# A two-layer graph network on one core: step 2's exponentials and search passes one slot later in the period

## The chip, the core and the metric

The kernel runs on one core of one Trainium2 chip. The metric is the device time of one execution in microseconds (us). The engines are TensorE (PE, with its weight loads PEld), VectorE (DVE), ScalarE (ACT), GpSimd (POOL) and SyncE (SP), which issues most of the DMAs.

## The reference, cut to what matters

The input is x (2708 x 256) and a sparse weighted adjacency matrix adj (2708 x 2708, about 0.3% of it nonzero, with the diagonal). Layer 0 is a graph convolution with a residual and a layer norm. Layer 1 has two attention steps with a nucleus (top-p) cut, beside two steps with the row-normalized adjacency:

```python
def _top_p_attention(X, W1, W2, W3):
    q = X @ W1.T @ W2.T
    k = X @ W3.T
    probs = jax.nn.softmax(q @ k.T, axis=-1)
    idx = jnp.argsort(-probs, axis=-1)
    sp = jnp.take_along_axis(probs, idx, axis=-1)
    cs = jnp.cumsum(sp, axis=-1)
    mask = ... # keep where cs - sp < 0.9
    A = probs * mask
    return A / A.sum(-1, keepdims=True)
R = (adj + eye) / row sums
for n in range(2):
    A = _top_p_attention(Xa, W1, W2, W3)
    Xf = R @ Xf
    Xa = A @ Xa
    Z = Z + Xf @ U1[n].T + Xa @ U2[n].T
x1 = layernorm(X + Z) * ln_g + ln_b
out = layernorm(X + x1)
```

## The kernel before

**Tiling.** The 2708 rows are 22 blocks (NB) of 128, the last one with 20 rows (EDGE). An attention step works on one block of 128 x 2708 exponentials at a time, which lie in one of four buffers es[0] to es[3].

**Stages.** Up to about 300 us layer 0 runs; from there to about 790 us step 1 of layer 1; from about 790 us step 2, the loop `for per in range(NB + 1)`, up to the last final stages. The change touches this loop alone.

**Step 2's loop.** One pass of the loop is called a period, and it is divided into NG = 6 slots (g = 0 to 5). Five blocks are under way in a period:

- block per - 1 (t_mul) is multiplied: `turn` (L520) transposes four 128 x 128 pieces of its kept exponentials on PE into a tr buffer (L526), ACT copies them into wT (L529, L532), and `products` (L552) multiplies them by ya on PE (L563), one slot behind;
- block per (b_dve) is cut on DVE: `last_level` (L959 to L962) takes the search's result, and `finish2` runs one long pass (L976), 20 maxima (L979), the sort (L576, L578), the level (L989 to L1004), five replacements (L1007) and the last pass (L1010); the kernel spreads it over the slots with yields;
- block per + 1 (b_act) is searched for its level on ACT: `try_act` runs a Relu pass (L922), a Sign pass (L925) and small operations (L928 to L938), and all of this twice, for k = 0 and 1. The last of them, L938, leaves the value that last_level reads a period later;
- block per + 2 (b_exp) gets its exponentials: `logits` multiplies queries by keys on PE into the one PSUM buffer lg (L506), in three parts (1024, 1024 and 660 columns), and `exps2` takes the exponential of each on ACT (L818, for the first part also L821 and L822);
- block per + 3 gets the first part of its logits in slot 5; `shift` (L815) takes its maximum on DVE at the start of the next period.

Between these, `r_units` (L718) issues the sparse product of the adjacency on PE (L730): 16 units a period, whose gathered rows POOL fetches by indirect DMA (L698). `r_out` and `arrive` on DVE (L753, L768) take up its results. From per = 10 on, r_units works on its second round, and from about per = 12 the final stages follow: the statistics on DVE (L1037), a Sqrt on ACT in slot 5 (L1087), the norm on ACT in slot 0 (L1047, after DVE's L1089 and L1090), POOL's scale and shift (L1062, L1063), the stores on SP (L1070).

**Order.** The schedule is written by hand: each engine runs its instructions in the order of the program, and waits only where an operand or a buffer asks for it. tr, wT and the accumulators have two buffers each; lg has one, so a logits call waits until the exponentials of the part before have read it. At per = 0 there is no turn and no b_exp; b_exp exists for per = 1 to 19, b_act for per = 0 to 20.

Of the kernel before, what the change touches and what calls it, by code (L numbers as in the profile page):

```python
# [52 lines left out]
def gnn_two_layer_kernel(ctx: ExitStack, tc: tile.TileContext, N, xT_d, x_d, adj_d, w0_d, b0_d,  # L53
# [71 lines left out]
    with fast:  # L125
        fast_path(fast, tc, c, flags, fint, xT_d, x_d, w0_d, b0_d, w1_d, w2_d, w3_d, u1_d, u2_d, g_d, b_d)
# [22 lines left out]
def fast_path(ctx, tc, c, flags, fint, xT_d, x_d, w0_d, b0_d, w1_d, w2_d, w3_d, u1_d, u2_d, g_d, b_d):  # L149
# [19 lines left out]
    def ps_acc(t=None):  # L169
        acc = ps.tile([P, CH], FP, tag="acc", name="acc")  # L170
        if t == NB - 1:
            nc.vector.memset(acc[:, :D + 1], 0.0)
        return acc
# [324 lines left out]
    def logits(s, t, i):  # L498


        p = rows(t)
        lg = ps_lg()
        cs = CHS[2 * i:2 * i + 2]
        for h, (a, b) in enumerate(cs):
            o = slice(DA * h, DA * h + DA)
            nc.tensor.matmul(lg[:p, h, :b - a], lhsT=q[o, t * P:t * P + p], rhs=keys[s][o, i, :b - a],  # L506
                             start=True, stop=True)
        a, b = cs[0][0], cs[-1][1]
        return lg.rearrange("p h n -> p (h n)")[:p, :b - a], a, b
# [42 lines left out]
    def products(keep):  # L552

        if len(before) > keep:
            p, ks, wT, y, acc = before.pop(0)
            for k in ks:
                kw = rows(k)
                if p < P:
                    o = EW * (k % 4)
                    nc.tensor.matmul(acc[o:o + p, :D], lhsT=wT[:kw, k % 4, :p], rhs=y[:kw, k, :],  # L560
                                     start=k < 4, stop=k >= NB - 4)
                    continue
                nc.tensor.matmul(acc[:p, :D], lhsT=wT[:kw, k % 4, :p], rhs=y[:kw, k, :],  # L563
                                 start=k == 0, stop=k == NB - 1)
# [34 lines left out]
    def exps1(t):  # L599

        p = rows(t)
        e = es[t % 4]
        nmax, srt = st1[t]
        z = small.tile([P, 2], FP, tag="z1", name="z1", bufs=3)
        st1[t] = (srt, z)
        h = 11 * P

        def part(i):
            if i == 0:
                nc.scalar.activation(srt[:p], srt[:p], AF.Exp, bias=nmax[:p], scale=1.0)  # L610
            a, b = ((0, h), (h, N))[i]
            nc.scalar.activation(e[:p, a:b], e[:p, a:b], AF.Exp, bias=nmax[:p], scale=1.0,
                                 accum_out=z[:p, i:i + 1])
        return part
# [103 lines left out]
    def r_units(n):  # L718
        for _ in range(n):
            s, m = r_queue[0]  # L720
            p = rows(m)
            if not r_now:
                r_now[:] = [ps_misc(), 0]
                if m + 1 < NB:
                    r_load(s, m + 1)
            acc, k = r_now
            a, y = r_in[s, m]
            kw = CW if k < CC else p
            rhs = v[:p, m, :] if s and k == CC else y[:kw, k, :]
            nc.tensor.matmul(acc[:p, :D], lhsT=a[:kw, k, :p], rhs=rhs, start=k == 0, stop=k == CC)  # L730
            r_now[1] += 1
            if k == CC:
                r_now.clear()
                r_queue.pop(0)
                r_in.pop((s, m))
                base = za_load(m) if s else None
                later[1].append(lambda s=s, m=m, acc=acc, base=base: r_out(s, m, acc, base))
# [44 lines left out]
    def e2(t):  # L782
        return es[(t + 2) % 4]
# [30 lines left out]
    def shift(b, lg):  # L814
        nc.vector.tensor_reduce(b.nmax, lg[:, :P], AX.X, ALU.max, negate=True)  # L815

    def exps2(b, i, lg, a, c_):
        nc.scalar.activation(e2(b.t)[:b.p, a:c_], lg, AF.Exp, bias=b.nmax, scale=1.0,  # L818
                             accum_out=b.all[:b.p, i:i + 1])
        if i == 0:  # L820
            nc.scalar.activation(b.half, b.nmax, AF.Identity, bias=part_of[:b.p], scale=0.5)  # L821
            nc.scalar.activation(e2(b.t)[:b.p, HC:2 * HC], lg, AF.Exp, bias=b.half, scale=0.5, accum_out=b.roots)  # L822
# [23 lines left out]
    part = exps1(0)  # L846
# [5 lines left out]
    part = exps1(1)  # L852
# [11 lines left out]
    for t in range(NB):  # L864
        acc = ps_acc(t)
        part = exps1(t + 2) if t + 2 < NB else None
# [4 lines left out]
        for g in range(NG):  # L871
# [5 lines left out]
            if b and g in (0, 2):  # L877
                lg = logits(1, b.t, g // 2)
# [239 lines left out]
    lg = logits(1, 3, 0)  # L1118
# [3 lines left out]
    for per in range(NB + 1):  # L1122
        n_r = units.get(per, 0)
        b_act = blocks.get(per + 1)
        b_dve = blocks.get(per)
        t_mul = per - 1 if per else None
        if per:
            accs[t_mul] = ps_acc(t_mul)
        masks = None
        b_exp = None  # L1130
        if per and per + 2 < NB:
            b_exp = blocks[per + 2] = Block(per + 2)
        for g in range(NG):
            n = n_r * (g + 1) // NG - n_r * g // NG
            now = later.pop(0)
            later.append([])
            if g == 0:
                if b_exp:
                    shift(b_exp, lg[0])
                r_units(n)  # L1140
            if t_mul == EDGE:
                if g == 0:
                    products(0)
                    edge_product(ya, accs[EDGE], e2(EDGE))
            elif per:
                turn(t_mul, g, ya, accs[t_mul], e2(t_mul))
            if b_exp and g == 3:
                lg = logits(1, b_exp.t, 2)
            if g == NG - 1 and 3 < per + 3 < NB:
                lg = logits(1, per + 3, 0)  # L1150
            if g:
                r_units(n)
            if b_exp and g == 1:
                lg = logits(1, b_exp.t, 1)
            if t_mul != EDGE:
                products(1 if per else 0)
            if b_exp and g in (0, 1, 3):
                exps2(b_exp, (g + 1) // 2, *lg)
            if b_act:
                for k, part in {0: ((0, 0),), 1: ((0, 1), (0, 2), (0, 3)), 2: ((1, 0),), 3: ((1, 1), (1, 2), (1, 3))}.get(g, ()):  # L1160
                    try_act(b_act, k, part)
            if g == 0:
                if b_dve:
                    last_level(b_dve)
                    masks = finish2(b_dve)
                    next(masks)
                final_slot(0)
                if per > 1:

                    t = t_mul - 1  # L1170
                    base = za_load(t)
                    later[0].append(lambda t=t, base=base: arrive(t, base, accs.pop(t), ras.pop(t)[:rows(t)]))
            elif masks:
                next(masks, None)
                if b_exp and g == 5:
                    begin_search(b_exp)
            for f in now:
                f()
            if g:
                final_slot(g)  # L1180
# [388 lines left out]
```

## Time and profile before

| what | value |
| --- | --- |
| median of 3 runs | 1396.02 us (1394.66 to 1401.23) |
| the profiled execution's own time | 1395.44 us |
| its span, first to last instruction | 1393.4 us |
| granted PE clock, mean | 0.966 |
| step 2's loop, first L976 to last L976 | 800.29 to 1345.34 us |
| a period of it, early (954.03 to 978.49) | 24.46 us |
| a period of it, late (1239.23 to 1266.03) | 26.80 us |
| L922 and L925 on ACT | x43 of 2641 ns, x42 of 2643 ns |
| L818 on ACT | x66, median 1114 ns |
| L506 on PE | x528, median 590 ns |

A profile is taken from one execution. Times in it are microseconds from the start of its span. A row of the timeline has start, duration, engine, line, operation, tiles out<-in, shape and count, and in square brackets the idle time before it and what ended that. A row of the waits has who waited, for whom, the total in us, how often, and the longest. Busy shares are means over the whole span.

### The profile page before, as it was taken

To read this page: it belongs to the slowest core of one execution; us is meant where nothing else is said; L and a number is where in the kernel's file an instruction comes from. 1 tells how busy PE (TensorE), PEld (TensorE's weight loads), DVE (VectorE), ACT (ScalarE), POOL (GpSimd) and SP (SyncE) were. 2 spreads that over 40 slices of the span, in tenths; PEclk is the share of its full clock that TensorE was granted. 3 is DMA by queue.
4 is the path that set the end of the run, shared out by engine and by line. 5 is a ranking of instruction groups with operands and counts; after the bars stand their busy time and mean duration, and the time that the engine had idled before them with its cause. 6 is when DMAs were issued, how large, how long until landed. Compare 5 with 4: busy or idle time off the path is not lost.

```text
span 1393.4 us, 18921 instructions
## 1 busy us (share of the span) xinstructions
PE 1279.4 (92%) x5788; PEld 898.7 (64%) x5788; DVE 1044.1 (75%) x3482; ACT 743.9 (53%) x1340; POOL 645.0 (46%) x595
## 2 busy tenths in 40 slices
PE   8999999988999999999998849999998988898884
PEld 6877877833567666666666437777665766566662
DVE  2544545865888887776751379999999988999996
ACT  1000000035455555555554438888887887899951
POOL 1000000014544532775555286776734757677870
PEclk9999999999999999999999879999999999999997
DMA  6544544512222110232223245545432544345351
GB/s 184 179 152 151 164 147 150 165 36 66 67 91 65 52 56 9 88 101 63 65 64 94 84 132 156 159 146 156 138 98 88 158 137 128 114 147 177 123 146 36
DMA packets 92830, 157.94 MB, mean 113 GB/s; under 512 B 16356, under 2 KB 65196, under 8 KB 92720
## 3 DMA queue, kind: packets, MB, share of 16 engines
q1 hardware_dynamic: 66434, 100.59, 22.7%
q0 software_dynamic: 20544, 51.17, 13.1%
q10 hardware_dynamic: 5742, 4.89, 1.3%
q8 instruction: 48, 0.79, 0.2%
q14 instruction: 62, 0.51, 0.1%
HBM read 125.33 MB, written 31.26 MB: 112 GB/s over the span
## 4 chain that ended last, share of the span: by engine, by line
PE 55%; DVE 36%; issue 3%; ACT 3%; another core or an unknown queue 1%; POOL 1%; DMA 0%; ACTq 0%; DVEq 0%; POOLq 0%
PE acc L563 16%; PE acc L255 15%; PE lg L506 6%; DVE cand L979 6%; DVE w L1007 5%; PE tr L526 5%; DVE e L1010 4%; DVE w L976 4%; PE misc L677 3%; DVE srt L576 3%; DVE spare L578 3%; PE acc L649 2%; PE misc L427 2%; PE acc L461 2%; PE misc L422 2%
## 5 line engine op out<-in xcount | busy, mean ns | idle before, releaser
L529 ACT COPY wT<-tr 128x512 f32<-128x512 f32 (+2 forms) x258 | 131.9, 518 | 242.0 <-PE tr L526 158.6
L563 PE MATMUL acc<-ya,wT 128*128 128x256 f32 (+1 forms) x924 | 235.8, 396 | 12.3 <-ACT wT L529 8.8
L563 PE MATMUL acc<-x,wT 128*128 128x256 f32 (+1 forms) x924 | 233.0, 391 | 6.6 <-ACT wT L529 6.6
L698 POOL DMA_INDIRECT yg<-yf_d,ix x154 | 192.6, 1251 | 95.3 <-PE misc L730 50.2
L698 POOL DMA_INDIRECT yg<-v_d,ix x154 | 194.8, 1265 | 85.5 <-PE tr L526 35.2
L563 PEld LDWEIGHTS acc<-x,wT 128*128 128x128 f32 (+1 forms) x924 | 166.5, 191 | 88.0 <-issue 48.5
L563 PEld LDWEIGHTS acc<-ya,wT 128*128 128x128 f32 (+1 forms) x924 | 172.2, 194 | 67.9 <-issue 26.4
L255 PE MATMUL acc<-y,adj_t 128*128 128x257 f32 (+1 forms) x924 | 208.8, 382 | 0.0
L365 POOL DMA_INDIRECT adj_t<-in_adj,ix x154 | 171.8, 1116 | 50.8 <-issue 39.9
L255 PEld LDWEIGHTS acc<-y,adj_t 128*128 128x128 f32 (+1 forms) x924 | 171.7, 189 | 33.8 <-issue 10.2
L730 PE MATMUL misc<-yg,adj_t 128*128 128x256 f32 (+1 forms) x660 | 174.4, 398 | 13.5 <-DVE v L753 7.0
L506 PE MATMUL lg<-k,q 64*128 64x512 f32 (+3 forms) x528 | 152.5, 601 | 26.9 <-ACT e L822 24.4
L526 PE MATMUL tr<-ident,e 128*128 128x128 f32 (+2 forms) x946 | 150.5, 279 | 19.3 <-DVE e L1010 18.9
L730 PEld LDWEIGHTS misc<-yg,adj_t 128*128 128x128 f32 (+1 forms) x660 | 118.5, 193 | 60.1 <-issue 20.7
L526 PEld LDWEIGHTS tr<-ident,e 128*128 128x128 f32 (+2 forms) x946 | 115.3, 142 | 61.8 <-issue 21.4
L332 POOL DMA_DIRECT2D part_d<-e x1 | 0.6, 573 | 294.5 <-DVE e L331 294.5
L569 DVE MAX8 cand<-e 128x8 f32<-128x170 f32 (+1 forms) x352 | 88.1, 319 | 38.5 <-ACT e L513 28.3
L922 ACT ACTIVATE w<-e,st 128x2708 f32<-128x2708 f32 (+1 forms) x43 | 113.5, 2640 | 0.0
L925 ACT ACTIVATE w<-e,st 128x2708 f32<-128x2708 f32 (+1 forms) x42 | 111.0, 2643 | 0.1
L438 ACT COPY x1T<-tr 128x256 f32<-128x256 f32 (+1 forms) x22 | 8.0, 364 | 192.1 <-PE tr L437 192.1
L979 DVE MAX8 cand<-w 128x8 f32<-128x136 f32 (+1 forms) x440 | 93.5, 284 | 0.8
L576 DVE MAX8 srt<-spare 128x8 f32<-128x128 f32 (+3 forms) x264 | 81.3, 308 | 9.1
(230 smaller groups left out, 1791.7 us busy)
## 6 DMA issues: line engine op xcount, KB each, us to landing
adj_t<-in_adj SPq DMA_DIRECT2D x44, 704.0 KB
adj_t<-adjc_d SPq DMA_DIRECT2D x44, 448.0 KB
adjc_d<-adj_t SPq DMA_DIRECT2D x22, 256.0 KB
base<-za_d SPq DMA_DIRECT2D x41, 128.0 KB
adjc_d<-adj_t SPq DMA_DIRECT2D x22, 192.0 KB
xt<-in_x ACTq DMA_DIRECT2D x21, 128.0 KB
x_d<-x SPq DMA_DIRECT2D x21, 128.0 KB
x1b_d<-xb SPq DMA_DIRECT2D x21, 128.0 KB
```

The costliest lines, as they stand in the source:

```text
L255: nc.tensor.matmul(acc[:p, :n], lhsT=halves[k // KH][:kw, k % KH, :p], rhs=y[:kw, k, :n], start=k == 0, stop=stop and k == NB - 1)
L365: nc.gpsimd.indirect_dma_start(out=a[:CW, i, :], out_offset=None, in_=adj_rows, in_offset=bass.IndirectOffsetOnAxis(ap=ix[:CW, m, i:i + 1] ...
L506: nc.tensor.matmul(lg[:p, h, :b - a], lhsT=q[o, t * P:t * P + p], rhs=keys[s][o, i, :b - a], start=True, stop=True)
L526: nc.tensor.transpose(tr[:kw, k % 4, :p], e[:p, k * P:k * P + kw], ident[:p, :p])
L529: nc.scalar.copy(wT[:, :full, :p], tr[:, :full, :p])
L563: nc.tensor.matmul(acc[:p, :D], lhsT=wT[:kw, k % 4, :p], rhs=y[:kw, k, :], start=k == 0, stop=k == NB - 1)
L576: nc.vector.max(dst[:p, i:i + 8], src[:p])
L698: nc.gpsimd.indirect_dma_start(out=y[:CW, i, :], out_offset=None, in_=rows_d, in_offset=bass.IndirectOffsetOnAxis(ap=ix[:CW, m, i:i + 1], ...
L730: nc.tensor.matmul(acc[:p, :D], lhsT=a[:kw, k, :p], rhs=rhs, start=k == 0, stop=k == CC)
L922: nc.scalar.activation(scr[:b.p, :N], e, AF.Relu, bias=b.nz, scale=b.l[k], accum_out=b.relu)
L925: nc.scalar.activation(scr[:b.p, :N], e, AF.Sign, bias=b.nz, scale=b.l[k], accum_out=b.sign)
L979: nc.vector.max(cand[:p, 8 * i:8 * i + 8], w[:p, SEG2 * i:SEG2 * (i + 1)])
```

## The change

In step 2's loop, the second part of the logits and its exponentials go from slot 1 to slot 2, and the third part from slot 3 to slot 4. The search's passes on ACT go from slots 0, 1, 2 and 3 to slots 1, 2, 3 and 4. The first part of the exponentials stays in slot 0, and the first part of the logits for the block after stays in slot 5. Within a slot the places stay: logits part 2 (the second) stands behind r_units, part 3 (the third) before them.

```diff
-            if b_exp and g == 3:
+            if b_exp and g == 4:
                 lg = logits(1, b_exp.t, 2)
             if g == NG - 1 and 3 < per + 3 < NB:
                 lg = logits(1, per + 3, 0)
             if g:
                 r_units(n)
-            if b_exp and g == 1:
+            if b_exp and g == 2:
                 lg = logits(1, b_exp.t, 1)
             if t_mul != EDGE:
                 products(1 if per else 0)
-            if b_exp and g in (0, 1, 3):
-                exps2(b_exp, (g + 1) // 2, *lg)
+            if b_exp and g in (0, 2, 4):
+                exps2(b_exp, g // 2, *lg)
             if b_act:
-                for k, part in {0: ((0, 0),), 1: ((0, 1), (0, 2), (0, 3)), 2: ((1, 0),), 3: ((1, 1), (1, 2), (1, 3))}.get(g, ()):
+                for k, part in {1: ((0, 0),), 2: ((0, 1), (0, 2), (0, 3)), 3: ((1, 0),), 4: ((1, 1), (1, 2), (1, 3))}.get(g, ()):
                     try_act(b_act, k, part)
```

## The prediction

> **What bounds the kernel now.** I read the page's busy table first, then the waits of VectorE (DVE) and TensorE (PE) in the stretch that the change touches (step 2's loop, about 794 to 1345 us), then single periods of that loop in the timeline.
>
> The page's table names PE as the busiest engine, which is a mean over stages:
>
> ```profile
> PE 1279.4 (92%) x5788; PEld 898.7 (64%) x5788; DVE 1044.1 (75%) x3482; ACT 743.9 (53%) x1340; POOL 645.0 (46%) x595
> ```
>
> Busy time by stage (columns: length, then busy us and count for PE, weight load, DVE, ACT and POOL, clock, DMA), for one early and one late period, each from one L976 to the next:
>
> ```profile
> 954.03:978.49 24.46, 23.18 (x113) 17.11 (x112) 23.45 (x80) 20.01 (x34) 17.75 (x14) 1.00 0.52 152
> 1239.23:1266.03 26.80, 23.94 (x113) 17.12 (x112) 25.62 (x90) 24.94 (x41) 21.09 (x18) 1.00 0.47 148
> ```
>
> The early period is 24.46 us, DVE busy 23.45; the late one, with the final stages in it, 26.80, DVE 25.62. What is left of DVE's time is some 1 us of short gaps inside its own chain of small operations, so the waits decide. DVE's, all of them, from 830 to 1350 us (total, times, longest):
>
> ```profile
> DVE e L1010 <- remote: 6.3, 1, 6.3
> DVE nmax L815 <- PE tr L526: 2.4, 1, 2.4
> DVE part L1004 <- DVE part L1002: 1.7, 3, 0.8
> DVE bulk L999 <- remote: 1.6, 1, 1.6
> DVE w L1007 <- DVE part L1004: 0.5, 1, 0.5
> DVE qs L994 <- DVE qs L993: 0.3, 1, 0.3
> ```
>
> In 21 periods DVE waits once for PE and never for ACT. PE's waits between 830 and 1345 us are the reverse:
>
> ```profile
> PE lg L506 <- ACT e L822: 19.9, 17, 4.9
> PE tr L526 <- DVE e L1010: 18.9, 10, 5.9
> PE acc L563 <- ACT wT L529: 8.8, 11, 1.8
> ```
>
> PE waits for ACT and for DVE. The chain that ended last agrees: between 900 and 1000 us it holds DVE lines and 3.5% of "issue", with no PE line among the large ones. **DVE bounds this loop.**
>
> How near are the others? ACT in the late stretch, and the DVE lines that need its result:
>
> ```profile
> 1263.40 0.19 ACT L938 ACTIVATE st<-st 128x1 f32<-128x1 f32 x1
> ...
> 1267.49 0.58 ACT L529 COPY wT<-tr 128x512 f32<-128x512 f32 x1 [1.52 <-PE tr L526]
> 1268.08 1.28 ACT L818 ACT_TABLE_LOAD   x1
> ```
>
> ```profile
> 1264.83 0.21 DVE L959 SCALAR_TENSOR_TENSOR st<-st 128x1 f32<-128x1 f32 x1
> ```
>
> ACT's last search result (L938) ends at 1263.59; DVE asks at 1264.83: a margin of **1.24 us**. PE starts the next block's transposes at 1266.80, 2.93 us after L1010 ended (1263.87), without waiting for it; it returns after 26.64 us (1293.44), DVE after 26.79. So late in the loop three engines run almost abreast. Early, L938 ends at 972.20 and L959 starts at 977.30: 5.1 us of margin.
>
> **What the Trainium skill says.** "Trainium Architecture — The Big Picture", Inside one NeuronCore: engines have their own instruction streams and meet only at semaphores. The trace agrees: a stalled PE (1.71 us at lg L506 in each late period) costs DVE nothing. "TensorE: Matmul & The Clock Gate", What's actually happening: about 3.4 us without work halves PE's clock. The trace shows it: after the 3.44 us wait at 1127.45 the clock is 0.51 from 1128 to 1132. "Runtime: NRT & Kernel Launch", Instruction fetch mechanics: each engine's instructions come by DMA in 16 KiB blocks. The page's q8 (48 packets, 0.79 MB, some 16 KB each) fits; that the stalls on "remote" are such fetches is my guess, no row proves it.
>
> **The change part by part.** DVE's, POOL's and SP's orders are unchanged, so no DMA issue moves in its queue; only PE and ACT are reordered.
>
> *PE, 19 periods (per 1 to 19).* Part 1 of the logits (two matmuls, 1.06 us of PE) goes from slot 1, just ahead of products, to slot 2, still behind the r_units; part 2 (1.06 us) from slot 3 to slot 4. Nothing is added. Today part 1 waits for L822 to free the one lg buffer: 0.3 us in each early period, 1.7 in each late one, 4.9 at 1191.95. After, a whole slot (products 1.73, transposes 0.44, r_units 1.3: 3.5 us) stands between; late, PE would reach it at 6.85 us after the first transposes, L822 has ended at 5.10. This wait goes. The next late ones are the first block of block per+3 in slot 5, which comes one slot after exps2's third part instead of two, and products waiting for wT.
>
> *ACT, 21 periods.* The four passes go one slot down: L922 (2.63), L925 (2.64 and 1.2 of small ones), twice. The sum is the same, and exponentials stay on either side of the Sqrt as before, so the table loads of 1.28 us stay as many. In front of L938 now stand five wT copies instead of four. Worked in order for a late period, from PE's first transpose: copy ends 1.28, table 2.58, exps2 part 0 5.10, norms (L1047, four) 7.07, copy 7.54, Relu 10.27, copy 10.73, exp 11.83, Sign and small 15.64, copy 16.1, Relu 18.83, copy 19.3, exp 20.1, Sign and small 24.0. Before, by the trace, L938 ends at 1290.23 - 1266.80 = 23.4. **L938 comes 0.6 us later** against PE's start.
>
> *PE in that same period:* products 0 to 5.1, turn 2, r_units 6.85, part 1 to 7.9, products 1 to 9.6, turn 3 and two r_units 11.1, products 2 to 12.8, turn 4 and part 2 to 14.4, r_units 15.7, products 3 waits for its wT until 16.1 and ends 17.9, turn 5, then lg waits for exp part 2 until **20.1**: about 1.9 us. Then lg, r_units, products 4, r_units: about 25.3 to 26.2 us against 26.64 today. Its stall moves from slot 1 to slot 5 and the total shrinks by 0.4 to 1.3 us a period. PE gets nearer to DVE, until it waits for L1010. Once the lag is gone, L1047 waits some 0.9 us for DVE's L1090, now that no Relu covers it; L938 is then at 25.0 after the first transpose, and DVE asks at 27.5: margin 2.5.
>
> *Early,* PE would find the slot 5 buffer free (exp part 2 ends at about 969.8, PE arrives at 970.1), and L938 moves from 972.2 to about 974.0 against 977.3. ACT's idle 4.2 us per period hides that. In the first period with its half clock (turn at 830.07) I get L938 at 853.6 against L959 at 854.36: 0.7 of margin left.
>
> *POOL and stores.* The norms run 2.7 us earlier, so L1062 waits less (1.3 to 1.4 us late), and the gathers behind it on POOL and the stores behind it on SP may start earlier. PE doesn't wait for gathers here, so that pays nothing.
>
> *The sum.* 19 x (0 on DVE) + 21 x (0 on DVE) = **0**. PE's 19.9 us of stall was already hidden: it turns into waiting for L1010. From below: all DVE waits that any engine could free are the 2.4 us at L815. At that moment (1181.8 to 1184.2) PE ("issue" 0.33 and 0.82) and ACT stand still too and its lg had been done since 1177.7, so I count none. From above: see the second rival. Against the profiled execution: span 1393.4, its own time 1395.44, 2.0 us around it; the median of the runs, 1396.02, is 0.6 above it. I forecast **1395.6 us**.
>
> **The rivals.** 0.5%, 7 us, is about what a measurement of this kernel can tell from no change; the runs shown span 6.6.
>
> *PE's stalls were the bound (faster).* For: 92% busy, 26.64 against DVE's 26.79 late. If all waits on L822 came back: 1395.4 - 19.9 = 1375.5; if only those of the late periods (11.8 us from 1185), 1383.7. Against: DVE doesn't wait for PE in these periods.
>
> *DVE begins to wait for ACT or PE at L959 or L815 (slower).* L938 ends ACT's work of a period, now behind a transpose copy that PE delivers one slot (some 4 us) later. It decides from a delay of 1.24 us in the late periods. If the whole slot came through, 4.0 - 1.2 = 2.8 us in each of some 8 late periods and 2.6 in the first two: 28 us, 1423. If half a slot, 0.8 x 8 = 6 us: 1402. For it: thin margins (1.1 to 1.3 at 1210 to 1264, 1.3 to 1.6 at 854 and 879). Against: my order of ACT gives 0.6, because ACT and not PE is the late one there, and PE loses lag.
>
> *The moved work changes nothing, but the unexplained stalls fall elsewhere.* 6.3, 1.6 and 2.4 us of DVE's waits (10.3 in all) follow no program wait and belong to this execution; other runs draw their own. 1390 to 1401.
>
> **How the numbers follow.** No effect by DVE's own chain, the stalls drawn again: 0.77 (its own range 1390 to 1401). DVE made to wait: 0.16, most of it between 1402 and 1423. PE the bound: 0.07. Range 1389 to 1405: the likeliest case and the lower end of the slower one. Faster by over 0.5% (below 1389) 0.07, same 0.77, slower (above 1403) 0.16.
>
> **What would show it.** Right: PE's wait on L822 almost gone from slot 2's logits; a wait of about 2 us at slot 5's lg in late periods, on L818; more time on L1010; periods still 24.4 and 26.8; no DVE wait on L938. Wrong: DVE waits at L959 or L815 repeating from period to period, a late period over 27.2, or periods under 24.3 and 26.5, which would say that DVE was not the bound.

## The result, and the profile after

The forecast was 1395.6 us, no measurable change. Measured, on one chip and seven executions each: before 1396.95 us (1394.66 to 1406.85), after **1408.1 us** (1405.06 to 1411.87), ratio **1.0068** (95% 1.0048 to 1.0088): slower by more than 0.5%. The profiled execution of the changed kernel took 1408.1 us, its span is 1406.2.

Later comparisons fell on five chips, and that turned out to be half of the answer. On four of them the kernel before takes 1373 to 1375 us, and on the three of these where the changed kernel itself ran, the change costs nothing. On the fifth the kernel before takes 1403 us; whether that is the first chip again is not known. So two questions have to be kept apart: what the change does to the schedule, and what makes it cost time on one chip and not on another.

The busy line of the page after, which answers to the one shown of before:

```profile
PE 1294.6 (92%) x5788; PEld 911.0 (65%) x5788; DVE 1044.6 (74%) x3482; ACT 746.0 (53%) x1340; POOL 633.2 (45%) x595
```

DVE, ACT and POOL do the same work in the same time; PE is busy 15.2 us longer with the same 5788 instructions, which is a matter of its clock. Busy time by stage of the changed kernel, one early and one late period from L976 to L976 (columns as in the prediction):

```profile
958.42:983.28 24.86, 23.31 (x113) 17.24 (x112) 23.43 (x79) 20.24 (x34) 18.52 (x15) 1.00 0.52 155
1219.66:1247.78 28.12, 25.90 (x115) 18.70 (x115) 25.60 (x89) 25.12 (x41) 21.43 (x19) 0.94 0.45 141
```

The early period is about as before (24.86; its neighbours are 24.46 and 24.66). The late one is 28.12 instead of 26.80 with DVE's busy time unchanged at 25.60: 2.5 us without work on DVE, against 1.2 before. PE's clock is 0.94. Of the 12.8 us between the two spans, 1.9 lie ahead of the loop (the first L976 starts at 802.16 instead of 800.29), and 11.15 in it (first to last L976: 556.20 against 545.05); 9.25 of these are the eight late periods from 1133.14 to 1358.36 (225.22 us; before, 1129.37 to 1345.34, 215.97).

DVE's waits of the changed kernel, 830 to 1362 us (total, times, longest):

```profile
DVE e L1010 <- issue: 6.3, 1, 6.3
DVE st L959 <- ACT st L938: 5.2, 4, 1.4
DVE e L1010 <- remote: 3.3, 2, 1.8
DVE nmax L815 <- PE acc L563: 2.5, 1, 2.5
DVE e L1010 <- DVE w L1007: 1.5, 2, 1.4
```

The 6.3 us are the first period's and stood there before too. New is the second line: DVE waits four times for ACT's last search result, which it never did before. New as well are late stops of 1.8, 1.4 and 1.55 us at L1010, the last pass, though the replacements that it reads (L1007) had ended. By a stop I mean here and below that an engine stands still while, as far as the trace shows, everything that its next instruction needs is there. PE's waits in the same stretch:

```profile
PE tr L526 <- DVE e L1010: 23.5, 10, 5.9
PE lg L506 <- ACT e L818: 12.6, 7, 4.0
PE lg L506 <- ACT wT L529: 6.2, 4, 1.7
...
PE lg L506 <- issue: 1.7, 1, 1.7
```

The wait for L822 (19.9 us before) has gone, as the prediction said. The three lines on L506 have come in its place, 20.5 us in all: they are one and the same wait, slot 5's logits for the third exponential, which the profile books to whatever semaphore event it still finds.

The chain of waits that ended last, taken for 1190 to 1345 us alone, shows the change of regime best (each by line, cut at the right). First the changed kernel on the first chip, then the same kernel on a chip where it costs nothing (experiment 5):

```profile
by line: ACT w L922 13.0%; ACT w L925 11.9%; ACT e L818 9.1%; issue 8.3%; ACT wT L529 7.7%; PE misc L730 6.9%; ACT yg L1047 6.4%; PE acc L563 5.9%; another core or an unknown queue 4.6%; ACT L818 4.1%; PE lg L506 2.7%; DVE cand L979 2.6%; A
```

```profile
by line: DVE cand L979 15.9%; DVE w L1007 12.9%; DVE e L1010 11.9%; DVE w L976 11.9%; DVE srt L576 7.8%; DVE spare L578 7.7%; DVE bst L1037 5.1%; DVE h L768 4.3%; issue 3.7%; DVE mvs L1038 2.8%; DVE bulk L999 1.3%; DVE qs L993 1.1%; DVE qs 
```

On the first chip the chain of the late periods runs through ACT and PE; on the other one through DVE, as before. How that comes about is to be seen in one period of the first trace (ACT, then PE, then DVE; start, duration, what, and in brackets the idle time before it):

```profile
1293.80 0.19 ACT L922 ACTIVATION_READ_ACCUMULATOR w<-e,st 128x1 f32 x1
1297.95 0.58 ACT L529 COPY wT<-tr 128x512 f32<-128x512 f32 x1 [3.97 <-remote]
1298.43 0.82 ACT L818 ACTIVATE e<-lg,nmax 128x660 f32<-128x660 f32 x1
...
1303.04 0.19 ACT L938 ACTIVATE st<-st 128x1 f32<-128x1 f32 x1
```

```profile
1295.01 0.38 PE L526 MATMUL tr<-ident,e 128*128 128x128 f32 x2
1299.39 1.90 PE L506 MATMUL lg<-k,q 64*20 64x512 f32 x4 [4.00 <-ACT e L818]
1301.22 2.07 PE L730 MATMUL misc<-yg,adj_t 128*128 128x256 f32 x4
1303.09 1.06 PE L730 MATMUL misc<-v,adj_t 128*128 128x256 f32 x2
1303.94 2.64 PE L563 MATMUL acc<-ya,wT 128*128 128x256 f32 x8
```

```profile
1303.26 0.22 DVE L959 SCALAR_TENSOR_TENSOR st<-st 128x1 f32<-128x1 f32 x1 [1.43 <-ACT st L938]
```

ACT stands still for 3.97 us, from 1293.98 on, ahead of slot 4's wT copy, whose transposes had ended at 1290.90 and whose buffer the products had left at 1290.47. The third exponential stands behind that copy and ends at 1299.25; PE has been waiting for it since 1295.39 and starts slot 5's logits at 1299.39. Then PE works at half clock: r_units take 2.07 and 1.06 us and products 2.64 (1.13, 0.59 and 1.89 at full clock in the period before). The search's result L938 stands on ACT behind that same copy, so it is late by the stop itself, and DVE, which wanted it at 1301.83, waits 1.43 us. The half clock acts one period later: PE starts the next transposes at 1307.28, 6.4 us after L1010 had ended, and L938 makes DVE wait again, 1.26 us at 1331.16, though ACT has no such stop in that period.

Of the four waits for L938, that last one alone comes through PE. The waits that end at 1106.44, 1189.10 and 1303.26 follow a stop of ACT in their own period: 2.40 us ahead of slot 3's copy at 1098.03, 3.23 and 3.97 ahead of slot 4's at 1183.80 and 1297.95. **L938 itself has moved behind slot 4's copy**; in the order of before it stands ahead of it. That counts here: from 1129 us on, in all six traces with stops that are kept, ACT's stops at a wT copy fall ahead of the copies of slots 4, 5 and 0 only.

### The profile page after: what moved, and what is told of

Same layout as the page of the kernel before. It is cut to its first block, busy times and chain, and to the rows that moved or that the text cites. A ratio compares the mean times of both kernels' runs of the same rounds, so it can differ in the third digit from the quotient of the medians.

```text
span 1406.2 us, 18884 instructions
## 1 busy us (share of the span) xinstructions
PE 1294.6 (92%) x5788; PEld 911.0 (65%) x5788; DVE 1044.6 (74%) x3482; ACT 746.0 (53%) x1340; POOL 633.2 (45%) x595
## 4 chain that ended last, share of the span: by engine, by line
PE 56%; DVE 28%; ACT 10%; issue 3%; another core or an unknown queue 1%; DMA 0%; SPq 0%; ACTq 0%; DVEq 0%
PE acc L563 16%; PE acc L255 15%; PE lg L506 6%; DVE cand L979 4%; PE tr L526 4%; DVE w L1007 4%; DVE w L976 3%; DVE e L1010 3%; PE misc L677 3%; DVE srt L576 2%; DVE spare L578 2%; PE acc L649 2%; ACT w L922 2%; PE misc L427 2%; ACT w L925 2%
## 5 line engine op out<-in xcount | busy, mean ns | idle before, releaser
L698 POOL DMA_INDIRECT yg<-yf_d,ix x154 | 187.7, 1219 | 103.2 <-PE misc L730 54.0
L698 POOL DMA_INDIRECT yg<-v_d,ix x154 | 185.5, 1205 | 96.2 <-PE tr L526 40.4
L563 PEld LDWEIGHTS acc<-ya,wT 128*128 128x128 f32 (+1 forms) x924 | 176.8, 198 | 58.2 <-issue 17.7
L730 PE MATMUL misc<-yg,adj_t 128*128 128x256 f32 (+1 forms) x660 | 187.0, 420 | 13.8 <-DVE w L1007 6.3
L365 POOL DMA_INDIRECT adj_t<-in_adj,ix x154 | 173.9, 1129 | 51.2 <-issue 39.9
L506 PE MATMUL lg<-k,q 64*128 64x512 f32 (+3 forms) x528 | 151.8, 602 | 27.5 <-ACT e L818 12.6
L730 PEld LDWEIGHTS misc<-yg,adj_t 128*128 128x128 f32 (+1 forms) x660 | 125.6, 204 | 64.6 <-issue 30.7
L922 ACT ACTIVATE w<-e,st 128x2708 f32<-128x2708 f32 (+1 forms) x43 | 113.9, 2648 | 0.0
```

The source lines that it names most:

```text
L365: nc.gpsimd.indirect_dma_start(out=a[:CW, i, :], out_offset=None, in_=adj_rows, in_offset=bass.IndirectOffsetOnAxis(ap=ix[:CW, m, i:i + 1] ...
L698: nc.gpsimd.indirect_dma_start(out=y[:CW, i, :], out_offset=None, in_=rows_d, in_offset=bass.IndirectOffsetOnAxis(ap=ix[:CW, m, i:i + 1], ...
L922: nc.scalar.activation(scr[:b.p, :N], e, AF.Relu, bias=b.nz, scale=b.l[k], accum_out=b.relu)
```

## The experiments

The kernels of one group were timed on one chip, with the kernel before beside them. Ratios are to the kernel before on that chip.

| kernel | before on that chip, us | ratio (95%) |
| --- | --- | --- |
| 1 logits only | 1374.48 | 1.0346 (1.0318 to 1.0375) |
| 2 search only | 1374.48 | 0.9991 (0.9980 to 1.0003) |
| 3 slot 5's logits last | 1374.48 | 1.0002 (0.9991 to 1.0014) |
| 4 norms first | 1374.48 | 0.9998 (0.9986 to 1.0009) |
| 5 the changed kernel | 1373.56 | 0.9995 (0.9983 to 1.0006) |
| 6 transposes eight times | 1373.56 | 1.0002 (0.9990 to 1.0014) |
| 7 third part back | 1373.56 | 1.0001 (0.9990 to 1.0011) |
| 8 Relu behind the exponential | 1373.56 | 1.0007 (0.9994 to 1.0020) |
| 9 before, delay 1.1 us | 1403.02 | 1.0018 (0.9999 to 1.0036) |
| 10 after, delay 1.1 us | 1403.02 | 1.0106 (1.0068 to 1.0143) |
| 11 before, delay 2.6 us | 1403.02 | 1.0093 (1.0071 to 1.0115) |
| 12 after, delay 2.6 us | 1403.02 | 1.0185 (1.0158 to 1.0213) |
| 13 the changed kernel | 1373.56 | 0.9986 (0.9975 to 0.9997) |
| 14 as 8 | 1373.56 | 0.9993 (0.9983 to 1.0003) |
| 15 before, as 9 | 1373.56 | 1.0016 (1.0006 to 1.0027) |
| 16 after, as 10 | 1373.56 | 1.0034 (1.0024 to 1.0044) |
| 17 the changed kernel | 1373.58 | 0.9985 (0.9974 to 0.9995) |
| 18 as 8 | 1373.58 | 1.0009 (0.9998 to 1.0020) |

### 1 to 4: which part of the change

Three theories after the first trace. **L**: slot 5's logits stand one slot behind the third exponential instead of two, PE waits there, its clock halves, and its next period starts late. **S**: the search's passes one slot later make L938 late for DVE by themselves. **P**: the norms (L1047), which the change frees from the Relu pass ahead of them, start POOL's work earlier, and that disturbs DVE at L1010. The expectations of 1 to 4 reckon in us from a kernel before of 1397; it took 1374.48 on this chip, so their ratios are what can be compared.

**1. Logits only:** the changed kernel with the search back in slots 0 to 3.

```diff
-  for k, part in {1: ((0, 0),), 2: ((0, 1), (0, 2), (0, 3)), 3: ((1, 0),), 4: ((1, 1), (1, 2), (1, 3))}.get(g, ()):
+  for k, part in {0: ((0, 0),), 1: ((0, 1), (0, 2), (0, 3)), 2: ((1, 0),), 3: ((1, 1), (1, 2), (1, 3))}.get(g, ()):
```

> The changed kernel's logits and exponentials (second and third part in slots 2 and 4), but the search's passes in slots 0 to 3 as before. Theory L (the slot 5 logits come one slot after the third part's exponentials, which stand at the end of ACT's chain; PE stalls there, its clock halves, the next block starts late): ACT's order now puts the whole search ahead of the third exponential, by the traced durations 24.0 us after PE's first transpose where the changed kernel has 20.1, so the slot 5 wait grows to about 5 us and a late period to about 29 us; also early periods slow down to about 26; 1410 to 1435 us. Theory S (the last search result L938 comes too late for DVE): L938 is as early as before, 1397. Theory P (the norms run ahead of the Relu, POOL's gathers fall elsewhere and DVE's last pass waits[...]): norms are behind the Relu as before, 1397.

Measured 1420.8 us, 1.0346, more than theory L's 1.009 to 1.027 (1410 to 1435 over 1397). DVE's and PE's waits, 790 to 1400 us:

```profile
DVE bulk L826 <- ACT e L818: 16.6, 16, 1.7
DVE nmax L815 <- PE lg L506: 15.6, 16, 1.5
```

```profile
PE lg L506 <- ACT e L818: 42.3, 18, 3.0
```

With all four search passes ahead of it, the third exponential is the last thing that ACT does for the block, and PE waits for it in every period. DVE then waits twice: at L826, which adds up the exponentials' sums, and at L815, which reads slot 5's logits. The loop takes 578.3 us instead of 531.9, early periods 27.3, late ones 30.6. So a late third exponential can bind the loop, directly through L826 and by way of slot 5's logits, about half and half. The place of the search decides whether it does: moving the search along with the exponentials is what keeps the change near level.

**2. Search only:** the kernel before with the search in slots 1 to 4 (the reverse of the diff above).

> The changed kernel's search passes (slots 1 to 4), but logits and exponentials as before (slots 1 and 3). Theory L: the third exponential ends about 16.9 us after PE's first transpose, before PE comes to the slot 5 logits, so no stall there: 1394 to 1399. Theory S: L938 as late as in the changed kernel, 1404 to 1408. Theory P: norms 2.7 us earlier as in the changed kernel, L1010 waits some 5 us in all, about 1402.

Measured 1373.91 us, 0.9991; DVE waits for nothing in the loop (531.9 us), late periods 26.8. Theory S falls where there are no stops: L938 a slot later is free there, as forecast. On a chip with stops this kernel, which also has L938 behind slot 4's copy, was not run, so what each of the two moves costs there is not separated.

**3. Slot 5's logits last:** the changed kernel with `lg = logits(1, per + 3, 0)` moved behind slot 5's r_units and products.

```diff
-            if g == NG - 1 and 3 < per + 3 < NB:
-                lg = logits(1, per + 3, 0)
             if g:
                 r_units(n)
...
             if t_mul != EDGE:
                 products(1 if per else 0)
+            if g == NG - 1 and 3 < per + 3 < NB:
+                lg = logits(1, per + 3, 0)
```

> The changed kernel with one move: the slot 5 logits (first part of block per+3) behind slot 5's r_units and products instead of ahead of them. Theory L: r_units and products 4 (3 us) fill the wait, the clock stays at 1.00, the next transposes start about 2 to 4 us earlier: 1394 to 1400, late periods 26.8. Theory S: as the changed kernel, 1405 to 1410. Theory P: 1402 to 1408.

Measured 1374.69 us, 1.0002: no wait for L818 is left on PE, DVE waits once for 1.0 us at L815. I took this as proof of L at the time. It isn't one, since the changed kernel itself is level on that kind of chip (experiment 5).

**4. Norms first:** the kernel before with the first Relu behind the norms in slot 0.

```diff
-  {0: ((0, 0),), 1: ...
+  {1: ((0, 1), (0, 2), (0, 3)), ...
             if g == 0:
...
                 final_slot(0)
+                if b_act:
+                    try_act(b_act, 0, 0)
```

> The kernel before with one move on ACT: in slot 0 the norms (L1047) ahead of the first Relu pass (L922) instead of behind it; POOL's scale and shift and the gathers behind them are released 2.7 us earlier, as in the changed kernel. Theory P: L1010 waits several times for 1 to 2 us, 1400 to 1403. Theories L and S: 1397, within 2.

Measured 1375.15 us, 0.9998, with no stop at L1010. Theory P falls, on a chip without such stops at least.

### 5 to 8: the changed kernel where the kernel before takes 1373 us

**5. The changed kernel, unaltered.**

> The changed kernel itself, to have its ratio, its profile and its stalls beside the next three on one chip. Theory L (the logits for the block after stand one slot behind the third exponential, PE waits there, its clock halves, and the next period's first block comes late): ratio 1.005 to 1.010, late periods 28.1 to 29.4 us, PE waiting for L818 at L506 1.2 to 3.0 us in most late periods, half clock behind the long ones. Rival R (the difference comes from stalls on nothing that the program waits for, the L1010 waits on remote of the first profile): these waits would not come back in the same place, and the ratio would fall under 1.004.

Measured 1372.27 us, 0.9995: **no difference**, against every theory of a loss that comes with the order alone. Rival R was nearest: the stops at L1010 don't come back. DVE waits for nothing at all between 830 and 1330 us, and the loop takes 531.9 us. PE still waits 1.70 us for L818 in each late period; it simply has the time. A late period of this trace on ACT, DVE and PE:

```profile
1215.25 0.19 ACT L938 ACTIVATE st<-st 128x1 f32<-128x1 f32 x1
```

```profile
1218.07 0.21 DVE L959 SCALAR_TENSOR_TENSOR st<-st 128x1 f32<-128x1 f32 x1
```

```profile
1190.43 0.66 PE L526 MATMUL tr<-ident,e 128*128 128x128 f32 x4 [0.44 <-DVE e L1010]
```

L938 ends 25.0 us after PE's first transpose and 2.6 us before DVE asks. These are the prediction's 25.0 and 2.5. PE reaches the next block 0.44 us before DVE releases it.

What differs between the chips is the stops. The names "remote" and "issue" don't measure them, since an ordinary wait whose event is missing from the trace is booked there too (the two of 4.2 us on ACT in the trace of before are such). Counted directly, DVE stands idle between its first and last L976 for 13.8 us in the first trace of before, 24.2 in that of after, and 0.0 in experiments 5 and 17. That accounts for the loop's length: 545.05 and 556.20 us with stops, 531.7 to 531.9 without (the changed kernel in 5, 13 and 17, and kernels 2 and 4, which are the kernel before with one edit). On ACT, wT copies stand still although their transposes and their buffer are ready (over 0.3 us at a time) for 15.3 us in 8 places before, 31.3 in 14 after, and nowhere in 5 and 17. The chip at 1403 has both kinds again (13 to 17 us on ACT's copies).

Two more things tell the traces apart. The stops are not drawn at random: in all six traces that have them DVE stands 6.3 to 6.6 us ahead of the first period's L1010, and 1.0 to 2.5 us in the small operations L999 to L1007 at per = 11. And these six traces hold 11741 to 12099 semaphore events, the fourteen without stops 20059 to 20100. The executions compared here were recorded too (each has a span and a clock), so **that the recording itself makes the stops is a rival that nothing here tests.**

**6. Transposes eight times:** the changed kernel with the two transposes of slot 5 repeated, to fill PE's wait.

```diff
-        for k in ks:
+        for k in list(ks) * again:        # again = 8 in slot 5, else 1
             kw = rows(k)
             nc.tensor.transpose(tr[:kw, k % 4, :p], e[:p, k * P:k * P + kw], ident[:p, :p])
```

> The changed kernel with the two transposes of slot 5 done 8 times over, so that PE has some 1.5 us more work just ahead of the logits where it waits 1.2 to 3.0 us. If the wait alone makes the period long (its length, whatever PE does in it), filling it leaves the time as it is where it is no longer than 1.5 us: the ratio stays that of the changed kernel, 1.005 to 1.010. If the halved clock behind the wait is a good part (r_units and products 1.2 to 1.5 us longer in a late period than at full clock, in about 9 late periods, so 11 to 13 us), PE stays at full clock and the ratio falls to between 0.999 and 1.003. If PE's work were what bounds the period, 20 x 1.5 us more would give 1.02 or more.

Measured 1373.66 us, 1.0002. PE's wait for L818 shrinks from 11.9 to 1.0 us in all, and nothing else happens. As the changed kernel is level there, this says only that 1.5 us more of PE work a period is free, so PE doesn't bind there; the clock's share it couldn't show.

**7. Third part back:** the changed kernel with the third part of logits and exponentials in slot 3 (`g == 3`, and `exps2` in slots 0, 2 and 3).

> The changed kernel with the third part of logits and exponentials back in slot 3; the second part stays in slot 2, the search in slots 1 to 4. Theory L: the third exponential stands ahead of the search's last two passes again and one slot further from slot 5's logits; PE's wait there goes, late periods back to 26.8, ratio 0.998 to 1.002. If the move of the second part were the cause instead (fewer slots between second and third part, PE now waiting for the second exponential in slot 3): late periods stay over 28 and the ratio at 1.005 to 1.010.

Measured 1372.82 us, 1.0001: level, like its base. PE waits 11.8 us in all for L818 here too, now for the second exponential. Inconclusive for the same reason as 6.

**8. Relu behind the exponential:** the changed kernel with the search's second Relu in slot 4, behind the third exponential. PE's order is untouched.

```diff
-  3: ((1, 0),), 4: ((1, 1), (1, 2), (1, 3))
+  4: ((1, 0), (1, 1), (1, 2), (1, 3))
```

> The changed kernel with the search's second Relu pass (2.64 us on ACT) in slot 4 behind the third exponential instead of slot 3 ahead of it; PE's order is untouched, the third part of logits stays in slot 4. Theory L in its ACT form (the wait at slot 5's logits is ACT being late, so work in front of the third exponential counts): the third exponential ends 2 to 2.6 us earlier, the wait falls from 1.2 to 3.0 us to under 0.7, ratio 0.998 to 1.003. If what counts is PE's place alone (one slot from the third logits to slot 5's, with the exponential between them), PE still waits some 1 us or more and the ratio stays at 1.005 to 1.010.

Measured 1373.32 us, 1.0007, and PE's wait at slot 5's logits has gone altogether. That settles what the wait of 1.70 us is made of: ACT's 2.64 us Relu pass ahead of the exponential, not PE's order.

### 9 to 12, 15 and 16: a delay at the place that hurt

If the first chip's stops on ACT are what makes the change cost time, an artificial one should do it too. Kernels 9 and 10 have one more ACT pass of about 1.1 us in periods 12 to 19, directly ahead of the wT copy before the third exponential (slot 3 before, slot 4 after), 11 and 12 one of 2.6 us.

```diff
             elif per:
+                if g == 4 and 12 <= per < 20:                  # before: g == 3
+                    nc.scalar.activation(scr[:b_act.p, :1024], e2(b_act.t)[:b_act.p, :1024],
+                                         AF.Sign, bias=b_act.nz, scale=b_act.l[1])   # 11, 12: all N
                 turn(t_mul, g, ya, accs[t_mul], e2(t_mul))
```

> The kernel before with one more ACT pass over 1024 columns (about 1.1 us, its result is not used) in periods 12 to 19, directly ahead of the wT copy that stands before the third exponential (slot 3). It imitates an ACT stall at the place that hurt in the slow trace. Theory M (the change uses up a margin: before it, the third exponential ends 1.76 us ahead of slot 5's logits on PE, after it, 1.70 us behind, and PE's next period then starts 0.4 us ahead of need): the margin of 1.76 covers 1.1, ratio 0.999 to 1.002. Rival N (both kernels stand a delay equally well, and the loss on the first chip came from more stalls in the changed program, not from less margin): the same ratio as the changed kernel with this pass, within 0.002.

> The changed kernel with the same pass of about 1.1 us in periods 12 to 19, directly ahead of the wT copy before the third exponential (slot 4). Theory M: PE's wait at slot 5's logits grows from 1.70 to 2.8 us, its clock halves behind it (some 1.5 us more), of which 1.4 us of slack is taken: 0.5 to 1.2 us in each of 8 periods, 4 to 10 us, ratio 1.003 to 1.007, late periods about 27.3 to 28. If the clock stays full: 1.000 to 1.002. Rival N: as the kernel before with this pass, within 0.002.

> The kernel before with one more ACT pass over all 2708 columns (about 2.6 us, unused) in periods 12 to 19, directly ahead of the wT copy before the third exponential. ACT's busy time in a late period goes from 24.9 to 27.5 us, over DVE's 26.8, so ACT bounds these periods at least: 8 x 0.75 = 6 us less the first period's slack. Theory M: ratio 1.002 to 1.006. Rival N: the same as the changed kernel with this pass, within 0.003.

> The changed kernel with the same pass of about 2.6 us. Theory M: PE waits over 3 us at slot 5's logits, the clock halves in each of these periods, PE's next start comes 2.64 + 1.5 - 1.4 = 2.7 us late: 8 x 2.7 = 22 us at most, ratio 1.008 to 1.017, with DVE waiting at L959 for L938 and at L815, as in the first trace of the changed kernel. Rival N: 1.002 to 1.006, as the kernel before with this pass.

These fell on the chip where the kernel before takes 1403 us, one with stops. With the same delay in both, the changed kernel is slower by 0.88% (1.0106 / 1.0018) and 0.91% (1.0185 / 1.0093); the intervals leave about 0.4% on either side. Rival N's equal ratios didn't come, but that alone doesn't refute it: how much of the 0.9% the change costs there without a delay, these four can't say, and on the first chip that was 0.68%. Theory M's numbers were too low for three of the four: 1.0106 against 1.003 to 1.007, 1.0185 against 1.008 to 1.017, and for the kernel before with the 2.6 us delay 1.0093 against 1.002 to 1.006. DVE's waits in kernel 12, 790 to 1380 us:

```profile
DVE e L1010 <- remote: 9.6, 2, 6.6
DVE st L959 <- ACT st L938: 9.5, 7, 3.3
DVE nmax L815 <- PE lg L506: 6.1, 4, 1.8
```

**15 and 16** are 9 and 10 again, on a chip without stops:

> The kernel before with the extra ACT pass of 1.1 us ahead of the wT copy before the third exponential, periods 12 to 19. On a chip without stalls: margin of 1.76 us, so 0.999 to 1.001. On one with stalls: 1.000 to 1.004 as measured.

> The changed kernel with the extra ACT pass of 1.1 us. On a chip without stalls, where the changed kernel itself is level: PE's wait at slot 5's logits 2.8 us, and if the clock halves behind it, late periods of 27.3 us and more, ratio 1.003 to 1.007; if the slack in PE's turn covers the delay, 0.999 to 1.002, and then the margin is not what the stalls used up. On a chip with stalls: 1.007 to 1.014 as measured.

Measured 1.0016 and 1.0034. The changed kernel itself is 0.9986 there (13), so the delay costs it 0.48%, some 6.6 us, and the kernel before 0.16%, 2.2 us (a little over the 1.001 expected). Here the base is known, and the first half of rival N, that both kernels stand a delay equally well, falls. Its second half, more stops in the changed program, is not touched by this. DVE's and PE's waits, 790 to 1340 us, first of the kernel before with the delay:

```profile
DVE st L959 <- ACT st L938: 1.7, 3, 0.7
```

```profile
PE acc L563 <- ACT wT L529: 19.9, 32, 1.9
PE lg L506 <- ACT e L822: 16.8, 18, 1.7
```

and of the changed one with it:

```profile
DVE st L959 <- ACT st L938: 5.6, 4, 2.2
```

```profile
PE lg L506 <- ACT e L818: 20.5, 8, 3.0
```

5.6 us in four waits for L938 is about what the first trace has (5.2 in four). The way there is not quite the same: this delay comes in every period, and at 1.1 us it is shorter than the margin of 2.6 at L938, so it needs PE to make it worse. How PE does that, in one of these periods:

```profile
1208.18 0.38 PE L526 MATMUL tr<-ident,e 128*128 128x128 f32 x2
1211.54 2.08 PE L506 MATMUL lg<-k,q 64*128 64x512 f32 x4 [2.98 <-ACT e L818]
1213.55 2.07 PE L730 MATMUL misc<-yg,adj_t 128*128 128x256 f32 x4
...
1219.68 0.60 PE L526 MATMUL tr<-ident,e 128*128 128x128 f32 x4
```

and the same stretch without the delay (the changed kernel, experiment 17):

```profile
1208.32 1.13 PE L506 MATMUL lg<-k,q 64*128 64x512 f32 x4 [1.70 <-ACT e L818]
1209.38 1.13 PE L730 MATMUL misc<-yg,adj_t 128*128 128x256 f32 x4
...
1213.96 0.66 PE L526 MATMUL tr<-ident,e 128*128 128x128 f32 x4 [0.43 <-DVE e L1010]
```

From slot 5's logits to the next block's transposes PE takes 8.14 us with the delay and 5.64, of which 0.43 are waiting, without: 1.3 us more of waiting ahead of the logits turn into 2.9 us more of work behind them. **The halved clock costs more than twice what the longer wait costs**, and both push PE's next start, and with it the next wT copy on ACT, past what DVE allows. That the clock is needed for it is argued from these rows; no run had the delay at full clock. The last four periods with the delay become 27.9 to 29.5 us with the changed kernel; before, with its third exponential a slot ahead, the same delay gives 27.0 to 27.9, and the half clock comes once in these periods, for some 3 us from 1224 on.

### 13, 14, 17 and 18: looking for the loss again

The changed kernel and the one with its wait taken away (as 8), twice more.

> The changed kernel itself, once more. If the loss needs the stalls that only some chips show: on a chip where the kernel before takes 1390 or more, ratio 1.004 to 1.010; where it takes about 1373, ratio 0.998 to 1.001. If the first result was a matter of that one chip or hour: 0.998 to 1.002 on any.

> The changed kernel with the second Relu pass behind the third exponential, once more: it took PE's wait at slot 5's logits away (none over 0.3 us in its trace). On a chip with stalls: if the loss goes through this margin, ratio 0.998 to 1.003 where the changed kernel has 1.004 to 1.010; if the loss comes from more stalls in the changed program as such, the ratio stays with the changed kernel's. On a chip without: 0.999 to 1.002 again.

> The changed kernel itself. Where the kernel before takes 1390 us or more (a chip with stalls): ratio 1.004 to 1.010 if the loss needs such stalls, 0.998 to 1.002 if the first result was a matter of that chip alone. Where it takes about 1373: 0.998 to 1.001.

> The changed kernel with the second Relu pass behind the third exponential. On a chip with stalls: 0.998 to 1.003 if the loss goes through the margin between the third exponential and slot 5's logits, as the changed kernel (1.004 to 1.010) if it doesn't. On one without: 0.999 to 1.002.

Both comparisons fell on chips without stops: 0.9986 and 0.9985 for the changed kernel, 0.9993 and 1.0009 for the other. Over three chips the change is thus level to 0.15% faster. The 2 us that two of the three give are not in the loop (531.7 us in both of these traces); I didn't look for them further. Whether the kernel of 8 would be level on a chip with stops is not known, since none of these runs fell on one. No version beat both kernels by more than these 2 us, which fits a loop that DVE bounds.

## Why the prediction was wrong

**The bound.** DVE bounds the loop: right without stops (531.7 to 531.9 us with the change and in kernels 2 and 4, no wait of DVE). On the first chip it holds for the early periods alone.

**PE's order.** The wait for L822 disappears and one "for exp part 2 until 20.1: about 1.9 us" comes at slot 5's logits: right, 1.70. A PE loop of 25.3 to 26.2 us: 26.4 (26.83 less 0.44 of waiting), a little over.

**ACT's order.** L938 at 25.0 us after the first transpose, a margin of 2.5: 25.0 and 2.6. Search only costs nothing (2): right.

**The step that failed** is the sum, "19 x (0 on DVE) + 21 x (0 on DVE)", where it put at nothing what ACT's stops do to L938 in the new order, together with the third rival's premise that the stops of "6.3, 1.6 and 2.4 us" merely "belong to this execution" and that "other runs draw their own". They go with the chip, or with the occasion, since no chip was used twice: the kernel before's fastest execution in the two comparisons with stops takes 1394.66 us, and all but one of its 188 executions in the other four take 1378.69 or less. They recur at the same places of the program. And what they cost depends on what stands behind them. The prediction noted that "in front of L938 now stand five wT copies instead of four" and priced the new order at 0.6 us, against a margin of 2.5; with a stop of 3.23 or 3.97 us ahead of that copy the margin is gone, and DVE waits for L938: 5.2 us in four waits where the sum has 0.

The same goes for the third exponential. Before, in a late period of the prediction's trace, it ended at 1259.70 and PE reached slot 5's logits at 1261.44: 1.7 us to spare. After, it ends 1.70 us too late. I had both numbers, priced the second one at full clock, and set it against PE's slack as if nothing else would ever delay ACT. The half clock, which I had shown in the prediction's own trace (0.51 after a wait of 3.44 us) and left out of the sum, follows when a stop makes that wait longer.

**The rival that came true** is the slower one, DVE waiting at L959 in the late periods, and 1408.1 lies in its 1402 to 1423. At L815 DVE waits no longer than before (2.5 us, once). Its reason was half right: L938 was delayed behind the very copy that it names, but by ACT's own stops and not by PE's transposes coming a slot later.

**How much is explained.** DVE's waits in the eight late periods are 11.2 us after (L959 on L938: 1.32, 1.43 and 1.26; L815: 2.46; L1010: 1.79, 1.38 and 1.55) and 2.4 before (L815). The difference, 8.8, is nearly all of the 9.25 us by which these periods grew. Of it, 4.0 us are waits for L938: 2.75 straight behind ACT's stops at slot 4's copy, 1.26 by way of slot 5's logits and the half clock. The other 4.7 us, at L1010, have nothing to do with either move as far as the trace shows: there DVE stops within its own chain. The first trace of before has none of it in these periods, but the kernel before with a delay (9) has a stop of 1.70 at the same L1010 where the changed kernel has its 1.79, so a single trace of each doesn't show that the change brings them. So less than half of the loss is traced to the change. Whether the changed kernel draws more stops (31.3 us on ACT's copies against 15.3, too) **stays open**, and so does their origin. My guess of instruction fetches found no support: the two instruction queues moved no packet during the longest stop of the trace of before (820.7 to 826.9), and q8 moved the same 48 packets on chips with stops and without. The prediction's 16 KiB blocks fit q8 alone; the packets of the other instruction queue, q14, are of 8 KB (62, 0.51 MB).

## What to carry to other kernels

A stall that moves off one place and turns up at another of the same length isn't a change of nothing: ask what now stands behind it, how far that is from its next deadline, and what a delay of the size of the largest unexplained stop in the trace would do at either place. Price a wait of PE with the clock behind it, not by its length alone. And before a level forecast is called right or wrong on half a per cent, run the unchanged pair on a second chip: the same two programs were 0.68% apart on one and level, or up to 0.15% apart the other way, on three others.

## What the runs showed of the hardware that I had not expected

**The same program took 1.6 to 2.1% longer in two of six comparisons.** The kernel before takes 1373.6 to 1374.5 us on four chips, 1397.0 and 1403.0 in the two other comparisons, with the same durations of instructions (L922 takes 2.64 us on either) and the same bytes moved. What is found there and not on the four are stops of DVE and ACT, of up to 6.6 us on DVE, that end on no wait of the program that the traces show. Each chip was used on one occasion, so chip and occasion can't be told apart.

**A wait of 1.70 us may or may not halve PE's clock.** The Trainium skill, "TensorE: Matmul & The Clock Gate", What's actually happening, says that the clock falls after an idle window of about 3.4 us, and that activity is watched in windows of 3413 ns which run freely. Half of that can be enough here. The changed kernel on the first chip, by stretches around a wait of 1.70 us that ends at 1211.97, then on the chip of experiment 17, around the same wait ending at 1208.32 (columns as in the prediction, PE first and the clock third from the end):

```profile
1210.00:1213.30 3.30, 1.60 (x8) 0.57 (x6) 3.26 (x7) 3.30 (x6) 2.39 (x4) 1.00 0.37 103
1213.30:1216.70 3.40, 3.40 (x9) 2.71 (x9) 2.43 (x7) 2.40 (x7) 3.10 (x2) 0.50 0.19 48
```

```profile
1206.00:1209.00 3.00, 1.30 (x8) 0.54 (x6) 2.86 (x11) 3.00 (x6) 2.39 (x3) 1.00 0.44 134
1209.00:1213.00 4.00, 4.00 (x21) 3.21 (x18) 3.96 (x7) 3.88 (x10) 3.09 (x4) 1.00 0.36 109
```

The half clock lasts 3.4 us, from 1213.3 to 1216.7, well after the wait has ended. The windows show in the traces: in each of the 20 that are kept, all changes of the clock lie on one grid of 3.41 us. On the first chip the whole wait lies inside one window of the grid (1209.9 to 1213.3, PE busy for 1.72 of 3.42 us); in experiment 17 an edge at 1207.1 divides it (PE busy for 2.56 and 2.17 us). Over step 2 of the 20 traces (800 to 1345 us) I count 2898 windows at full clock. In 96 of them PE is busy for less than 40%, and half clock follows every one; it follows 66 of the 179 between 40 and 62%, and none of the 2623 above. **So what counts is how idle PE is within one window**, and about half of it is where either can happen: the first trace has another wait of 1.70 us inside one window, ending at 1266.95, without half clock behind it. Even 2.97 us (experiment 16) didn't do it each time: five of six such waits were followed by half clock, the one that ended at 1127.48 was not.

**The loop may lock to that window.** In experiment 1, where PE waits in each period, six early periods in a row took 27.27 to 27.32 us and four late ones in a row 30.42 to 30.63; 8 and 9 of the page's windows of 3413 ns would be, by estimate, 27.30 and 30.72, so the early ones fit and the late ones only nearly. That is an observation; nothing was run to test it.
